# Four transformer layers in one launch: spreads of gates by sixteen strided writes, products finished in the next layer, and transposes through DRAM

## The chip, the cores and the metric

The kernel runs on one core of a Trainium2 chip. Its engines are TensorE (PE: matrix products; PEld is the load of the stationary operand), VectorE (DVE), ScalarE (ACT), GpSimd (POOL) and SyncE (SP, which here issues nearly all DMAs). The metric is the device time of one launch in microseconds, the median over several runs. For this kernel a difference under 0.3%, some 4.2 us, can't be told from none.

## The reference

Eight layers, four of attention and four of feed-forward, act one after another on 4096 tokens of 128 numbers, in float32, each on the normalized tokens, with its result added to them. Cut to what the change touches:

```
x = L0_attn_x                                   # 8 x 512 tokens x 128
x = x + L0_attn(_layernorm(x), ...)
x = x + L0_ffn(_layernorm(x), ...)              # each of 8 heads of 16 numbers picks 2 of 16 experts
x = x + L1_attn(...); x = x + L1_ffn(...)       # linear attention; gated product, 256 chosen tokens
x = x + L2_attn(...); x = x + L2_ffn(...)       # 16 heads, softmax over the queries; 8 low-rank experts
x = x + L3_attn(...); x = x + L3_ffn(...)       # convolution of 21 taps; products of 4-bit numbers

def _L0_ffn_ref(x, ...):
    t = (x @ Wm + bm).reshape(-1, 16)
    topw, topi = top_k(softmax(t @ expert_emb), 2)
    hmid = gelu(einsum('td,edi->tei', t, W1) + b1)
    eo = einsum('tei,eio->teo', hmid, W2) + b2
    return (weighted sum of the two chosen eo).reshape(..) @ Wo + bo

def _L3_attn_ref(x, W1, W2, bias, table):       # 21 taps over time, one filter per channel
    return x @ W1 + causal_conv(x, table) @ W2 + bias

def _L3_ffn_ref(x, w_gate, w_up, w_down):       # fp4: blocks of 16 numbers, rounded to 8 levels
    h = silu(fp4(x) @ fp4(w_gate).T) * (fp4(x) @ fp4(w_up).T)
    return fp4(h) @ fp4(w_down).T
```

## The kernel before

The tokens stay in SBUF as eight blocks `x[0]` to `x[7]` of 512 tokens (four tiles of 128 tokens by 128 features; NB = 8, J = 4, TB = 512, P = 128, D = 128). The order of the instructions on every engine is the order in which the program writes them (`manual_schedule`); nothing is reordered afterwards. An engine that waits holds everything written behind it.

**Layer 0 (0 to 384 us).** After the attention (to about 101 us) come 128 units, one for each block b and expert e, sixteen per block. `first_half(b, e)` makes the hidden numbers: eight products on PE, and the GELU on ACT in two instructions (L569, 512 wide; L570, 1536 wide). `second_half(b, e)` makes eight products from them, DVE multiplies by the gate (L582, `pr`), and POOL adds `pr` to `acc` (L588). The gate of a token for an expert is one row of 512 numbers in DRAM (`gates[b]`); `spread(b, k)` (L550) brings four experts' rows into `gs`, 128 partitions, each head's rows repeated over its 16 partitions: eight DMAs of 128 KB, one per head. `gs` has three buffers, so a spread is issued by `fetch` as soon as four units have been used up. The program keeps eight DMA semaphores for such transfers in turn, so the issue of one waits for the eighth before it. The `choice` of a block (the two best experts and their weights, mostly DVE) runs beside the units of the block before and writes its gates to DRAM by four DMAs (L477). `finish(b)` multiplies the block's sum by `wo` and adds the result to `x[b]`: it is put at the fifth unit of the next block, and for the last block after all units; there the last `pr` goes into the product by itself.

**Layer 1 (384 to about 510 us).** A list of steps with offsets, applied to the blocks in turn (`run`).

**Layers 2 and 3 (516 to 1330 us) in 64 frames.** Frame n is one pair of heads of a block (eight frames per block) of layer 2's attention: `first_scores(n)`, `context(n-1)`, `weigh(n, 0)`, `scores(n, 1)`, `project(n)` (the queries and keys of n+2, the values of n+1 and the output of n-1 in 64-row halves, interleaved), `weigh(n, 1)`. Between two halves of `project`, the order is held by marks: an empty instruction on SP (L1523) that waits for one PE instruction and that another PE instruction waits for. In the frames of the set `moving` (9, 12, 17, 20) the plain 128-row functions `queries`, `output` and `values` stand for `project`. All other work is hung into the frames with `at(frame, hook, function)`. The hooks, in the order in which they run: S and P inside the first scores, V behind them, G behind the first weighing, D before the projections, E at the end. Hung in are the layer-2 experts (`put`, `load`, `products`, `back`, `add`), the norms of layer 2 (`new_xt`), the quantized weights of layer 3 (`rounded`, `turned_w`), and layer 3 block by block (`planned`): norm, 21 taps of the convolution (`conv_v` on DVE, L2009; `conv_s` as a product on ACT, L2023, and a sum on POOL, L2024), `quant_x`, `turn_x`, four gate steps, `quant_h`, `blocks_h` and `fetch_h` (h turned through DRAM, already in the kernel before), `down`. A block is "wide" for b from 0 to 4.

Turning by PE means four transposes into PSUM and a copy by ACT or DVE: `turn_` of `norm_steps` (L1472) for the tokens of layers 2 and 3, `turn_x` (L2089), `turned_w` (weights). `end()` (to 1392 us) does what is left of layer 3's last blocks.

Of the kernel before, what the change touches and what calls it, by code (L numbers as in the profile page):

```python
# [164 lines left out]
def body(ctx, tc, dram, spans, x_in, ib, it, ic, ei, out):  # L165
# [113 lines left out]

    def layer0():  # L280
# [7 lines left out]
        with ExitStack() as st:  # L288
# [7 lines left out]
            acc = once.tile([P, NB, TB], F32, tag="acc", name="acc")  # L296
# [46 lines left out]
            def scale(b, own=3):  # L343
                l0[b]["xn"] = xn = norm.tile([P, J, D], F32, tag="xn", name="xn")
                nb, rs = l0[b]["by"]
                scaled(xn, x[b], (nb, rs), own)
                for j in range(own, J):
                    r1, n1 = rs[:, j : j + 1], nb[:, j : j + 1]
                    nc.gpsimd.tensor_scalar(xn[:, j, :], x[b][:, j, :], r1, n1, ALU.mult, ALU.add)
# [89 lines left out]
            def exponentials(b):  # L439
                nc.scalar.activation(acc[:, b, :], depth[:, b, :], AF.Exp)  # L440

            def choice(b):


                d, ex = by_expert(depth, b), by_expert(acc, b)
# [43 lines left out]
            with (  # L489
# [8 lines left out]
                def run(stages, iterations):  # L498
                    for i in iterations:
# [20 lines left out]
                        (lambda b: scale(b, J), -1),  # L520
# [22 lines left out]
            def spread(b, k):  # L543

                gs = wp.tile([P, 4, TB], F32, tag="gs", name="gs", bufs=3)
                src = gates[b].rearrange("(h k e) t -> k h e t", h=8, k=4)[k]
                n = 2 if (b, k) == (0, 0) else 4
                for e in range(0, 4, n):
                    for hd in range(8):
                        nc.sync.dma_start(  # L550
                            gs[16 * hd : 16 * (hd + 1), e : e + n, :],
                            src[hd, e : e + n, :].unsqueeze(0).to_broadcast([16, n, TB]),
                        )
                return gs
# [18 lines left out]
            def second_half(b, e, hm, gs):  # L573
# [7 lines left out]
                pr = acc[:, b, :] if e == 0 else wp.tile([P, TB], F32, tag="pr", name="pr")  # L581
# [3 lines left out]
                if (b, e) == (NB - 1, 15):  # L585
                    l0[b]["last"] = pr
                elif e > 0:
                    nc.gpsimd.tensor_tensor(acc[:, b, :], acc[:, b, :], pr, ALU.add)  # L588

            def finish(b):  # L590
                terms = [(lambda j: acc[:, b, j * P : (j + 1) * P], f0["wo"])]
                if "last" in l0[b]:
                    terms.append((lambda j: cols(l0[b]["last"], j), f0["wo"]))
                add_to_residual(b, by_token(terms, None))
# [48 lines left out]
            with tc.manual_schedule():  # L643
# [36 lines left out]
                def second(n):  # L680
# [5 lines left out]
                    for _ in range(1 if n > 1 else 5):  # L686
                        side("V", n)

                for n in range(len(units) + 2):
                    first(n)  # L690
                    if n >= len(units):

                        banks["own"] = threes[0][:, 1 + n - len(units), :]
                        second(n)
                        banks.pop("own")
                        continue
# [3 lines left out]
                    if e == 4 and b > 0:  # L700
# [5 lines left out]
                finish(NB - 1)  # L706
# [124 lines left out]
    def layer1():  # L831
# [9 lines left out]
        with tc.tile_pool(name="l1", bufs=2) as wp, tc.tile_pool(name="l1c", bufs=1) as once:  # L841
# [372 lines left out]
            def chosen_put():  # L1214
# [13 lines left out]
                (project_kv, 0),  # L1228
                (z_turn, -7),
# [9 lines left out]
            with tc.manual_schedule():  # L1239
# [13 lines left out]
                nought = once.tile([P, J, D], F32, tag="nought", name="nought")  # L1253
# [152 lines left out]
    def late():  # L1406
# [11 lines left out]
        with tc.tile_pool(name="a2", bufs=2) as wp, tc.tile_pool(name="l3", bufs=1) as lp:  # L1418
# [3 lines left out]
            steps = {}  # L1422

# [6 lines left out]


            def norm_steps(b, dst, bias=None, part=(0, J)):
# [41 lines left out]

                return stats, scale, turn_, t
# [223 lines left out]
            class Rows:  # L1699
# [116 lines left out]
                def products(self, meanwhile, ahead):  # L1816
# [63 lines left out]
                    def last(k, d):  # L1880
# [11 lines left out]
                        for m, f in enumerate((nc.scalar.copy, nc.vector.tensor_copy)):  # L1892
# [33 lines left out]
                def back(self, js):  # L1926
                    if js[0] == 0:
                        self.rows = both("cg").rearrange("p (n d) -> p n d", d=D)
                    for j in js:
                        for k in range(2):  # L1930
                            n = 2 * j + k
                            at_ = 8 * self.b + n
                            nc.gpsimd.indirect_dma_start(
                                self.rows[:, n, :],
                                None,
                                slots_out[self.b],
                                bass.IndirectOffsetOnAxis(spots[:, at_ : at_ + 1], 0),
                            )
# [49 lines left out]
            def layer3(b, xp, tile_, part=(0, J), conv_bank="one", h_tag="h"):  # L1988
# [96 lines left out]

                def turn_x():
# [58 lines left out]
                def quant_h2_tile(i, j):  # L2145
                    sc, a = t["fh", i]
                    k = slice(22 * j, 22 * (j + 1))
                    h = tile_("h", h_tile)
                    fp4_round(lp, h[:, 2 * i + j, :], sc[:, k], a[:, k, :], 22)
# [76 lines left out]
                stats, scale, turn_, _ = norm_steps(  # L2226
                    b, lambda: xp()[:, pad + lo : pad + hi], "b3", part
                )
                stats2, scale2, _, t2 = norm_steps(b, None, None, part)
                return SimpleNamespace(t=t, **{k: v for k, v in locals().items() if callable(v)})  # L2230

            def planned(b, f0_):
# [7 lines left out]
                plan = [  # L2240
                    (1, "V", s.stats) if b == 1 else (0, "E", s.stats),
                    (1, "G", s.scale),
                    (1, "E", s.turn_),
                    (2, "D", lambda: s.conv_v(5)),
                ]
                if b == 0:
# [6 lines left out]
                        (3, "E", lambda: s.conv_s(15, 16)),  # L2253
                        (4, "E", lambda: s.conv_s(19, 20)),
                    ]
                else:
                    plan += [
                        (2, "V", lambda: s.conv_v(1, 2)),
                        (3, "V", lambda: s.conv_v(3, 4)),
                        (2, "G", lambda: s.conv_s(6, 7)),  # L2260
                        (2, "E", lambda: s.conv_s(8, 9, 10)),
                        (3, "G", lambda: s.conv_s(11, 12)),
                        (3, "E", lambda: s.conv_s(13, 14, 15)),
                        (4, "G", lambda: s.conv_s(16, 17)),
# [7 lines left out]
                    (6, "E", s.quant_x1) if early else (z - 2, "V", s.quant_x1),  # L2272
                    (z - 1, "V", s.quant_x2),
                    (z - 1, "E", s.turn_x),
                ]
                for j in range(J):
# [10 lines left out]
                    (h_ + 4, "V", lambda: s.quant_h2(1)),  # L2287
                ]
                if wide:
                    plan += [  # L2290
                        (z + 2, "E", lambda: s.blocks_h(0)),
                        (z + 3, "E", lambda: s.fetch_h(0)),
                        (z + 4, "E", lambda: s.blocks_h(1)),
                        (z + 5, "E", lambda: s.fetch_h(1)),
                        (z + 6, "E", s.down),
# [12 lines left out]
            for b in range(1, NB):  # L2308
                stats, scale, turn_, _ = norm_steps(b, new_xt(b), "lb")
                n = {1: 3, 2: 6, 3: 14, 4: 26, 5: 33, 6: 40, 7: 47}[b]  # L2310
                at(n, "V" if b < 4 else "E", stats)
                at(n + 1, "G", scale)
                at(n + 1, "E", turn_)
            start = [13, 20, 27, 34, 41, 48, 56]
            rows_after = {}
            for b in range(2):
# [10 lines left out]
                at(8 * b + 11, "E", lambda r_=r_: r_.back((0, 1)))  # L2327
                at(8 * b + 12, "G", lambda r_=r_: r_.back((2, 3)))
# [9 lines left out]
            def end():  # L2338
# [63 lines left out]
                B.quant_h2_tile(1, 0)  # L2402
                B.quant_h2_tile(1, 1)
# [5 lines left out]
            def weights_in_frames():  # L2409
# [20 lines left out]
                def turned_w(name):  # L2430
                    ps = bank()
                    w_ = wq[name]
                    if name == "down":
                        for i, at_ in thirds:
                            nc.tensor.transpose(
                                ps[:C3, i * P : (i + 1) * P], w_[:, at_ : at_ + C3], ident
                            )
                        wt["down"] = const.tile([P, 3, P], F32, tag="wd", name="wd")
                        nc.vector.tensor_copy(
                            wt["down"][:C3], ps[:C3, : 3 * P].rearrange("p (i n) -> p i n", i=3)  # L2440
# [237 lines left out]
```

## Time and profile before

| what | us |
|---|---|
| runs (three) | 1394.31, 1395.56, 1398.51 |
| median | 1395.56 |
| the profiled execution | 1393.95 |
| its span, first to last instruction | 1392.2 |
| layer 0 to the last unit's products | 0 to 383.6 |
| layer 1 | 386 to about 510 |
| 64 frames | 516 to 1330 |

The profiled execution is 1.7 longer than its span and 1.6 under the median. Reading: the busy table gives each engine's busy time and share of the span; the chain is followed back from the last instruction; a group's row has line, engine, operation, output and inputs, shape and count, then busy time, mean ns, and the idle time before it with what ended it. A window's row has start:end, length, the busy time of PE, PEld, DVE, ACT and POOL with instruction counts, the granted clock, the share of the DMA engines and GB/s. A timeline's row has start, duration, engine, line, operation, and in square brackets the idle time before and what ended it.

### The profile page before, as it was taken

Reading aid. Unit: us, or ns where it says so; the run is one execution under the profiler, and the core shown is the slowest. Engines: PE = TensorE matmul, PEld = TensorE weight load, DVE = VectorE, ACT = ScalarE, POOL = GpSimd, SP = SyncE. Lnnn points to the kernel's source line nnn. Section 1 sums busy time; section 2 is a strip of 40 time slices with the busy share of each in tenths; the row PEclk is TensorE's granted clock in tenths of the full one; section 3 lists DMA queues with packets and bytes.
Section 4 is the critical chain, followed back from the end, with each engine's and each line's share of the span. In section 5 each row is a group of like instructions: output and inputs, shape, how many; then the busy total and the mean of one; then the engine's idle time right before and its main releaser. Section 6 shows DMA issues by size and latency. Waiting matters only on the chain.

```text
span 1392.2 us, 33106 instructions
## 1 busy us (share of the span) xinstructions
PE 1327.5 (95%) x12935; PEld 706.1 (51%) x12935; DVE 1014.3 (73%) x2148; ACT 1014.6 (73%) x2060; POOL 642.4 (46%) x748
## 2 busy tenths in 40 slices
PE   7889999999989999999999999999999999999997
PEld 3762222222267655547447545555555545555576
DVE  6785556666467778863783778888788797887876
ACT  7869999999978656665684686787767867667632
POOL 6645666666632533330472353353443634424432
PEclk9999999999999999999999999999999999999999
DMA  5019999999681010031211101101011010010000
GB/s 180 1 27 139 141 126 127 132 127 133 85 272 32 28 40 24 16 108 33 60 31 38 45 2 22 30 2 33 20 22 24 9 33 20 19 27 9 2 8 16
DMA packets 100713, 78.14 MB, mean 56 GB/s; under 512 B 52717, under 2 KB 93581, under 8 KB 96206
## 3 DMA queue, kind: packets, MB, share of 16 engines
q1 hardware_dynamic: 98828, 72.10, 28.3%
q0 software_dynamic: 1152, 2.36, 0.6%
q8 instruction: 102, 1.67, 0.6%
q10 hardware_dynamic: 578, 1.57, 0.3%
q14 instruction: 53, 0.43, 0.1%
HBM read 59.03 MB, written 16.97 MB: 55 GB/s over the span
## 4 chain that ended last, share of the span: by engine, by line
PE 52%; ACT 22%; DVE 19%; issue 3%; POOL 2%; DMA 1%; SPq 1%; DVEq 0%; ACTq 0%; POOLq 0%
PE ps L250 41%; PE ps L1556 8%; ACT hm L570 6%; ACT ex L1635 5%; DVE nm L1629 5%; ACT hm L569 3%; ACT prod L2023 2%; PE ps L2206 1%; DVE fa L1395 1%; DVE acc L2009 1%; DVE s L732 1%; ACT h L389 1%; DVE fa L1379 1%; DVE fsc L1374 1%; ACT q L1517 1%
## 5 line engine op out<-in xcount | busy, mean ns | idle before, releaser
L1635 ACT ACTIVATE ex<-ps,nm 128x512 f32<-128x512 f32 x512 | 345.2, 687 | 172.6 <-DVE nm L1629 170.2
L1629 DVE TENSOR_REDUCE nm<-ps 128x2 f32<-128x1024 f32 x256 | 301.1, 1211 | 41.9 <-PE ps L250 41.5
L250 PE MATMUL ps<-q,k 64*64 64x512 f32 (+1 forms) x2240 | 258.3, 565 | 7.4 <-ACT ex L1635 5.4
L250 PE MATMUL ps<-ex,vs 128*64 128x512 f32 x1024 | 233.9, 599 | 1.1 <-DVE sm L1649 1.1
L1650 POOL TENSOR_TENSOR vs<-v,sm 128x256 f32<-128x256 f32 x128 | 78.6, 614 | 296.6 <-DVE sm L1649 269.6
L588 POOL TENSOR_TENSOR acc<-acc,pr 128x512 f32<-128x512 f32 x119 | 165.6, 1391 | 93.8 <-DVE pr L582 85.8
L1556 PE MATMUL ps<-xt,blob_a 64*64 64x512 f32 x912 | 207.8, 589 | 0.5 <-SPq L1523 0.5
L570 ACT ACTIVATE hm<-ps,blob_f 128x1536 f32<-128x1536 f32 x128 | 196.2, 1533 | 0.0
L582 DVE SCALAR_TENSOR_TENSOR pr<-ps,blob_f,gs 128x512 f32<-128x512 f32 x120 | 90.1, 750 | 93.7 <-PE ps L250 72.1
L250 PEld LDWEIGHTS ps<-q,k 64*64 64x64 f32 x2240 | 74.6, 132 | 150.5 <-ACT ex L1635 77.6
L250 PE MATMUL ps<-h,w 32*128 32x512 f32 x1024 | 148.3, 643 | 1.1 <-ACT hm L569 0.6
L250 PEld LDWEIGHTS ps<-ex,vs 128*64 128x64 f32 x1024 | 68.1, 137 | 152.9 <-issue 126.7
L250 PE MATMUL ps<-hm,w 128*32 128x512 f32 x1024 | 136.9, 607 | 2.3 <-DVE pr L582 2.2
L2024 POOL TENSOR_TENSOR acs<-acs,prod 128x512 f32<-128x512 f32 x96 | 124.0, 1292 | 23.9 <-ACT prod L2023 19.4
L1556 PE MATMUL ps<-blob_a,ct 64*64 64x128 f32 x1824 | 118.6, 269 | 0.0
L1556 PE MATMUL ps<-blob_a,xt 64*64 64x128 f32 x1824 | 118.6, 269 | 0.0
L1556 PEld LDWEIGHTS ps<-blob_a,ct 64*64 64x64 f32 x1824 | 106.3, 133 | 0.0
L1635 ACT ACTIVATION_READ_ACCUMULATOR ex<-ps,nm 128x1 f32 x512 | 104.9, 205 | 0.0
L1556 PEld LDWEIGHTS ps<-blob_a,xt 64*64 64x64 f32 x1824 | 103.0, 133 | 0.0
L569 ACT ACTIVATE hm<-ps,blob_f 128x512 f32<-128x512 f32 x128 | 88.0, 687 | 13.3 <-PE ps L250 13.2
L250 PEld LDWEIGHTS ps<-h,w 32*128 32x128 f32 x1024 | 41.0, 184 | 109.1 <-ACT hm L569 100.5
L1556 PEld LDWEIGHTS ps<-xt,blob_a 64*64 64x64 f32 x912 | 61.7, 133 | 32.2 <-issue 28.7
(373 smaller groups left out, 2204.5 us busy)
## 6 DMA issues: line engine op xcount, KB each, us to landing
gs<-gates SPq DMA_DIRECT2D x248, 128.0 KB, 7.4
ht<-turned_h SPq DMA_DIRECT2D x20, 180.0 KB, 3.0
turned_h<-hb SPq DMA_DIRECT2D x40, 88.0 KB, 2.3
blob_f<-in_f SPq DMA_DIRECT2D x1, 2560.0 KB, 9.0
blob_a<-in_a SPq DMA_DIRECT2D x1, 2056.0 KB, 13.5
x<-in_x SPq DMA_DIRECT2D x8, 256.0 KB, 5.8
gates<-turned SPq DMA_DIRECT2D x32, 64.0 KB, 4.7
slots_in<-nought SPq DMA_DIRECT2D x8, 256.0 KB, 4.8
```

Source lines behind the costliest of these rows:

```text
L250: nc.tensor.matmul(out_, lhs, rhs, start=start, stop=stop)
L389: nc.scalar.activation(hk, hk, AF.Sigmoid, bias=bi[:, k : k + 1], scale=sc[:, k : k + 1])
L569: nc.scalar.activation(hm[:, 0, :], p1, AF.Gelu, bias=bias)
L570: nc.scalar.activation(hm[:, 1:, :], p3, AF.Gelu, bias=bias)
L582: nc.vector.scalar_tensor_tensor(pr, po, f0["b2"][:, e : e + 1], gs, ALU.add, ALU.mult)
L588: nc.gpsimd.tensor_tensor(acc[:, b, :], acc[:, b, :], pr, ALU.add)
L1556: ins = nc.tensor.matmul(*args, **kw).ins
L1629: nc.vector.tensor_reduce(nm, ps, AX.X, ALU.max, negate=True)
L1635: nc.scalar.activation(ex[kt][:, i, :], ps[:, i, :], AF.Exp, bias=nm[:, i : i + 1], accum_out=sm[:, kt, i : i + 1],)
L1650: nc.gpsimd.tensor_tensor(vs[:, tiles, :, :], vs_[n][:, tiles, :].rearrange("p j (i n) -> p j i n", i=2), sm[:, tiles, :].unsqueeze(3).to_ ...
L2023: nc.scalar.activation(p, src, AF.Copy, scale=w)
L2024: nc.gpsimd.tensor_tensor(t["acs"], t["acs"], p, ALU.add)
```

## The change

- Layer 0's `spread`: all but the first become sixteen DMAs of 64 KB, the r-th of which writes partitions r, r+16, r+32, ..., one for each head, each with 8 KB.
- `finish` moves out of the units for blocks 2 to 7: block 2's runs behind the last unit, those of blocks 3 to 7 inside layer 1's list; `acc` of these lives in a pool that lasts longer. The last `pr` is added on POOL like the others. At the start one of four normalizations per block moves from ACT to POOL, and fewer side steps run beside the first two units.
- `in_blocks`: DVE transposes 32 by 32 squares of a 128x512 tile in place, four DMAs write the squares to DRAM in turned order, and one DMA fetches the whole. It replaces PE's transposes and ACT's copies for the tokens of layer 2 (seven blocks), the norm of layer 3 for blocks 2 to 4, and `turn_x` of the wide blocks; the three quantized weights are turned in the same manner. That is 18 runs. A new hook F, behind the second weighing and before E, issues the fetches.
- Taps 1, 2 and 5 of the convolution move, in most blocks, from DVE (`conv_v`) to ACT and POOL (`conv_s`): 19 of 30 taps.
- The gathers of the layer-2 experts' rows (`back`) are issued three before the projection, three at the end of that frame and two in the next; frames 11 and 19 join `moving`. The first copy of `ge` is DVE's.
- The wide blocks' quantizations are moved by a frame, part of the second half's with them; `blocks_h(1)`, `fetch_h(1)` and `down` come one or two frames later; `bounds` one earlier.

```diff
+    def finish(b):
+        wo = f0["wo"]
+        add_to_residual(b, by_token([(lambda j: cols(acc[b], j), wo)], None))
...
-            def scale(b, own=3):
+            def scale(b):
...
-                scaled(xn, x[b], (nb, rs), own)
...
+                scaled(xn, x[b], (nb, rs), 3)
...
-                n = 2 if (b, k) == (0, 0) else 4
-                for e in range(0, 4, n):
-                    for hd in range(8):
-                        nc.sync.dma_start(
-                            gs[16 * hd : 16 * (hd + 1), e : e + n, :],
-                            src[hd, e : e + n, :].unsqueeze(0).to_broadcast([16, n, TB]),
-                        )
...
+                else:
+                    for r in range(16):
+                        nc.sync.dma_start(gs[r::16, :, :], src)
...
-                if (b, e) == (NB - 1, 15):
-                    l0[b]["last"] = pr
-                elif e > 0:
...
+                if e > 0:
+                    nc.gpsimd.tensor_tensor(acc[b], acc[b], pr, ALU.add)
...
-                    for _ in range(1 if n > 1 else 5):
+                    for _ in range((4, 2)[n] if n < 2 else 1):
...
+                        if n == len(units):
+                            banks["own"] = threes[0][:, 0, :]
+                            finish(2)
...
-                    if e == 4 and b > 0:
+                    if e == 4 and 0 < b < 3:
...
-                finish(NB - 1)
...
+                (lambda b: b > 2 and finish(b), 3),
...
+            def in_blocks(src):
+                nc.vector.transpose(src, src)
+                far = tc.dram_tile([P, TB], F32, name=f"turned{len(fars)}")
+                fars.append(far)
+                to = far.rearrange("(c r) (j a s) -> a r j c s", c=4, j=J, a=4)
+                for a in range(4):
+                    nc.sync.dma_start(
+                        to[a],
+                        src[32 * a : 32 * (a + 1), :].rearrange("r (j c s) -> r j c s", j=J, c=4),
+                    )
+                return far
...
+                def blocks():
+                    t["far"] = in_blocks(t["xn"].rearrange("p j d -> p (j d)"))
+
+                def fetch():
+                    nc.sync.dma_start(dst(), t["far"])
...
+                def blocks_x():
+                    t["far"] = in_blocks(t["xq"])
+
+                def fetch_x():
+                    t["xt"] = xt = tile_("xt", block("xt3", 2))
+                    nc.sync.dma_start(xt, t["far"])
...
+                if 2 <= b <= 4:
+                    plan = [
+                        (-1, "E", s.stats),
+                        (0, "G", s.scale),
+                        (0, "E", s.blocks1),
+                        (1, "F", s.fetch1),
+                    ]
...
-                        (2, "V", lambda: s.conv_v(1, 2)),
                         (3, "V", lambda: s.conv_v(3, 4)),
-                        (2, "G", lambda: s.conv_s(6, 7)),
+                        (2, "G", lambda: s.conv_s(6, 7, 1)),
...
-                        (3, "G", lambda: s.conv_s(11, 12)),
+                        (3, "G", lambda: s.conv_s(11, 12, 2)),
...
-                        (4, "G", lambda: s.conv_s(16, 17)),
+                        (4, "G", lambda: s.conv_s(16, 17, 5)),
...
+                if wide:
+                    plan += [
+                        (z - 3, "V", s.quant_x1),
+                        (z - 2, "V", s.quant_x2),
+                        (z - 2, "E", s.blocks_x),
+                        (z - 1, "F", s.fetch_x),
+                    ]
...
-                        (z + 3, "E", lambda: s.fetch_h(0)),
-                        (z + 4, "E", lambda: s.blocks_h(1)),
-                        (z + 5, "E", lambda: s.fetch_h(1)),
-                        (z + 6, "E", s.down),
+                        (z + 3, "F", lambda: s.fetch_h(0)),
+                        (z + 5 + more, "F", lambda: s.fetch_h(1)),
+                        (z + 6 + more, "E", s.down),
...
-                n = {1: 3, 2: 6, 3: 14, 4: 26, 5: 33, 6: 40, 7: 47}[b]
+                n = {1: 3, 2: 5, 3: 14, 4: 27, 5: 34, 6: 41, 7: 48}[b]
...
-                at(n + 1, "E", turn_)
+                blocks, fetch = t_["in turn"]
+                at(n + 1, "E", blocks)
+                at(n + 2, "F", fetch)
...
-                at(8 * b + 11, "E", lambda r_=r_: r_.back((0, 1)))
-                at(8 * b + 12, "G", lambda r_=r_: r_.back((2, 3)))
+                at(8 * b + 11, "D", lambda r_=r_: r_.back((0, 1, 2)))
+                at(8 * b + 11, "E", lambda r_=r_: r_.back((3, 4, 5)))
+                at(8 * b + 12, "G", lambda r_=r_: r_.back((6, 7)))
...
-                    at(frame + 1, "E", lambda name=name: turned_w(name))
+                    at(frame + 1, "E", lambda name=name: raw.update({(name, 0): turned_w(name)}))
+                    at(frame + 3, "F", lambda name=name: fetch_w(name, raw[name, 0]))
...
-                moving = {8 * b + k for b in range(2) for k in (9, 12)}
+                moving = {8 * b + k for b in range(2) for k in (9, 11, 12)}
...
+                    hook(n, "F")
                     hook(n, "E")
```

## What was predicted

> **What bounds the kernel now.** I read the busy table first, then the chain that ended last, then windows inside two stages, then timelines of single waits. All times are microseconds.
>
> ```profile
> PE 1327.5 (95%) x12935; PEld 706.1 (51%) x12935; DVE 1014.3 (73%) x2148; ACT 1014.6 (73%) x2060; POOL 642.4 (46%) x748
> ...
> PE 52%; ACT 22%; DVE 19%; issue 3%; POOL 2%; DMA 1%; SPq 1%; DVEq 0%; ACTq 0%; POOLq 0%
> ```
>
> PE is busy 95% of the span and holds half of the chain, but ACT and DVE hold 41%, so the binding engine differs by stage. Windows (start:end, length, then PE, PEld, DVE, ACT, POOL busy, granted clock, DMA share, GB/s) separate layer 0's experts (first two rows) from the frames of layers 2 and 3 (last two):
>
> ```profile
> 220.00:260.00 40.00, 39.69 (x308) 9.76 (x304) 27.43 (x53) 38.59 (x37) 27.25 (x20) 1.00 0.99 130
> 260.00:300.00 40.00, 39.47 (x311) 9.61 (x307) 28.13 (x62) 38.35 (x39) 27.12 (x20) 1.00 0.99 129
> ...
> 880.00:905.00 25.00, 24.46 (x300) 14.81 (x300) 19.13 (x28) 19.28 (x50) 7.68 (x11) 1.00 0.12 32
> 1000.00:1025.00 25.00, 25.00 (x342) 14.44 (x338) 20.33 (x29) 20.06 (x51) 15.49 (x15) 1.00 0.01 2
> ```
>
> In the experts, PE's share counts waiting matmuls; ACT is at 96%, and the DMA engines at 99% with 129 GB/s: two resources are full at once. In the frames PE is full and nothing else is. Clock 1.00 everywhere.
>
> The experts' pace is ACT's pair per unit (a block and an expert, 128 of them); its one gap per block is a `finish`:
>
> ```profile
> L570 ACT ACTIVATE hm<-ps,blob_f 128x1536 f32<-128x1536 f32 x128 | 196.2, 1533 | 0.0
> L569 ACT ACTIVATE hm<-ps,blob_f 128x512 f32<-128x512 f32 x128 | 88.0, 687 | 13.3 <-PE ps L250 13.2
> ...
> 288.82 0.69 ACT L569 ACTIVATE hm<-ps,blob_f 128x512 f32<-128x512 f32 x1 [1.37 <-PE ps L250]
> ...
> gs<-gates SPq DMA_DIRECT2D x248, 128.0 KB, 7.4
> ```
>
> A unit is 2.07 (starts 288.82, 290.88, 292.95); with a finish ahead of it 3.48, so a finish costs 1.41. A block is 16 x 2.07 + 1.41 = 34.5.
>
> In a frame (base 10.64) PE's transposes lie between the last product of one step and the next:
>
> ```profile
> 886.72 0.49 PE L1556 MATMUL ps<-blob_a,xt 64*64 64x128 f32 x6
> 887.31 0.63 PE L1472 MATMUL ps<-blob_c,xn 128*128 128x128 f32 x4
> 887.87 1.95 PE L250 MATMUL ps<-q,k 64*64 64x512 f32 x16
> ```
>
> From the start of the last projection to the next scores is 1.15; where no transposes stand it is 0.32.
>
> **Transposes through DRAM.** Each run takes its PE transposes off the frame's end and adds a VectorE transpose of 128x512 (0.70, by L474, 702 ns), four writes and one or two fetches on SP. On PE, by the gaps around each: seven token runs of layer 2, 0.88 + 0.92 + 0.88 + 0.91 + 0.91 + 1.08 + 1.14 = 6.7; three norms of layer 3 at 1.05 = 3.15; five `turn_x`, 1.08 once and 0.45 four times (after `down`) = 2.9; three weights at 0.68 to 0.70 = 2.1. Together 14.85 for the 18 runs.
>
> What it costs back. (a) `fetch_x` sits at the new hook F, about 1.1 before the frame ends and, in frames 30, 37, 44, 51, behind another fetch of 256 KB on SP; such loads land 2.3 (weights by row) to 3.0 (`ht`) after issue, and the gate step wants the tile 1.34 into the next scores. Stall 0 to 1.1 each: 0 to 4.4, I take 2.5. (b) In frames 28, 35, 42, 49 two runs of writes stand on SP ahead of the marks (L1523) that order the next projection's two halves; DVE's `hb` transpose (0.88 at 876.49) ended about 8.4 into the frame, the mark is wanted at 9. Behind the late mark wait PE's second half, then `v` and the next `ex`. Eight issues of 0.42 to 0.46 are 3.5; 0.6 of cover and four of them already out leave 0 to 1.5 late: 0 to 6, I take 1.5, because the base frame has SP idle before. (c) DVE: 15 x 0.70 added, 19 taps taken off (19 x 0.927 = 17.6, L2009). So DVE gains in sum; but in frames 25 and 48 its instructions add to 13.3 and 13.0 (11.7 before) while PE needs about 11.8 there: 0 to 5, I take 2. (d) The taps go to ACT (0.718, L2023) and POOL (1.292, L2024); ACT's sum per frame rises to 12.1 in a few frames of 11.83, but its measured union is lower: 0 to 2, I take 1. The cover of (c) and (d) is PE's full frame; were it gone, 19 x 0.718 = 13.6 would show. (e) Frames 11 and 19 take the 128-row form (frames 12 and 20, of that kind, measure 11.04 against 10.64): +0.8. (f) Gathers moved around D, E and G: POOL has 4 to 6 idle per frame; 0.
>
> Small gains: the products' first copy `ge` moves to DVE, where ACT's late copy held PE (2.7 + 0.9 waited in two products): 0.9 to 3.6, I take 0.9. Frame 55 has 0.93 of PE gaps behind DVE (11.4 busy of 12.0), and loses two taps: 0.7.
>
> Frames: -14.85 - 0.9 - 0.7 + 2.5 + 1.5 + 2 + 1 + 0.8 = **-8.65**.
>
> **Finishes.** In-stage finishes for blocks 2 to 6 go: 5 x 1.41 = 7.05 if nothing else holds the block. Something does: the spreads, which take 8.16 of DMA per 1 MB (eight DMAs at 1.02) and stand still about 2.1 per block while the choice's weights are written, 4 x 8.16 + 2.1 = 34.7, already the block's length. The slack of a block's first spread before use is only 1.41, 1.74, 2.17 in blocks 4, 6, 7. With unchanged DMA rate the gain is that slack, 2; with faster spreads 7.
>
> **Sixteen-way spreads.** 496 DMAs of 64 KB replace 248 of 128 KB; each now writes partitions r, r+16, ... and has 8 packets of 8 KB instead of 16. SP: 0.465 per issue unblocked (199.77, 200.24, 200.69), 16 x 0.465 = 7.4 per spread, or 64 x 0.465 + 5.1 (choice) = 34.9 per block: as full as the DMA.
>
> ```profile
> SPq L550 <- DMA gs<-gates: 84.8, 129, 1.8
> SPq L550 <- DVE pr L582: 16.2, 13, 2.2
> ```
>
> SP now waits 129 times for an earlier DMA, so issue isn't the limit yet. What a packet will take decides: 0.366 when the queue was empty (200.36), 1.02 once full; the 7200-byte packets that spread one row over all 128 partitions at 12.3 to 14.7 kept 0.273, so rereading one source row isn't what slows them; the write into 16 neighbouring partitions is. A block has 64 such DMAs one after another, so the break-even is 64 x p + 2.1 = 34.7, p = 0.51. Bounds: p = 0.273 x 8192/7200 = 0.31 (then issue binds, full gain -7) and 1.02 (4 x 16.3 + 2.1 = 67.4 per block, +33 in each of 8). Between, half as many packets at a time through the same 128 GB/s give p = 0.512, and I take this one, since the rows show a shared rate: packets lengthened step by step as a queue filled. Stage: **-2**, from -7 to +5 near that value.
>
> [...] The trace shows no 8-packet DMA of this size. [...]
>
> **Layer 1 and the tail.** Five finishes now run inside layer 1: eight matmuls each, 0.89 of PE, in a stage where PE's first iterations have idle of 1.8 to 2.2: 5 x 0.89 = 4.5 less one hidden, **+3.5** (2.5 to 5). After the last unit PE ended at 383.63 and layer 1 began at 386.24, behind `finish(7)` waiting on POOL's sum (start 384.35): **-2.6** (-1.5 to -3.2). The fourth normalization per block on POOL instead of ACT (layer 0's start): 0, between -1 and +1. `bounds` and the layer-3 quantizations a frame earlier lie on DVE beside PE: counted in (c).
>
> **Sum.** -8.65 - 2 + 3.5 - 2.6 = -9.75, on the profiled 1393.95 gives 1384.2. The median of the runs is 1.6 above that execution, so 1385.8: **1386**.
>
> **Rivals.**
> 1. *Full feed and late fetches.* Stage 0, layer 1 +5, tail -2; frames -16.45 + 0.8 with (a) 4.4, (b) 3, (c) 5, (d) 2 = -1.25. Sum +1.75: 1395.56 + 1.75 = **1397**, no change. For: frames 25 and 48, and SP's marks behind eight issues; against: nearly every bound must be at its end. Chance 0.12.
> 2. *Slower side: eight packets at a time.* One mechanism: in the experts' stage, the packet time p on half the packets. Each 0.01 over 0.51 costs 64 x 0.01 = 0.64 per block, 5.1 in eight. At p = 0.53 the whole gain is gone, from 0.54 it is slower; the second DMA of a burst already had 0.576. At 0.55: 8 x (64 x 0.55 + 2.1 - 34.7) = +21 instead of -2, **1409**; at 1.02 some 1650. For: saturated rows show 1.02; against: fewer writers at a time. Chance 0.15.
> 3. *Faster spreads and hidden costs.* Stage -7, (a) to (d) a quarter of what I took (1.75 instead of 7): 1386 - 5 - 5.25 = **1376**. Chance 0.20.
> 4. My forecast: 0.53.
>
> About 0.3% (4.2) is what a measurement of this kernel can tell from no change. Faster: 0.53 and 0.20, 0.73 in all; same 0.12; slower 0.15. The range 1371 to 1404 takes in rivals 1 and 3 and the edge of 2; the likeliest case alone is 1380 to 1392.
>
> **What would show it.** Experts: windows with ACT above 39 of 40 and no 1.37 gaps mean -7; waits of `pr` on DMA of `gs`, and packets over 0.53, mean rival 2. Frames: the gap before first scores 0.32 instead of 1.15; PE idle at L2206 on the fetched tile is (a), at L1556 on SP (b), at L250 scores on DVE `nm` (c). Layer 1 should be about 3.5 longer. I am wrong if the frames together gain less than 3 or the stage moves by more than 7.

## The result, and the profile after

The changed kernel takes 1462.43 us (median of 6 runs, 1461.41 to 1467.46) against 1395.91 before (6 runs, 1394.31 to 1398.51): ratio 1.0482, 95% interval 1.0463 to 1.0500. It is slower by 67, where 1386 and a range of 1371 to 1404 were predicted. Split at the same places in both traces (from the second part of the first unit's GELU to the end of the last unit's products; from there to the first frame; 63 frames, each from its first `ps<-ex,vs` product to that of the next; what follows them). What lies ahead of the first row took 103.7 before and 103.1 after.

| stage, us | before | after | difference | predicted |
|---|---|---|---|---|
| layer 0's units | 279.9 | 341.0 | +61.1 | -2 |
| end of the units and layer 1 | 132.1 | 133.3 | +1.2 | +0.9 |
| frames | 814.2 | 820.3 | +6.1 | -8.65 |
| after the frames | 62.3 | 62.4 | +0.1 | 0 |

The page of the changed kernel, its busy table and the chain that ended last (shares by engine):

```profile
PE 1343.3 (92%) x12738; PEld 701.8 (48%) x12738; DVE 1008.2 (69%) x2165; ACT 1016.2 (70%) x2054; POOL 672.6 (46%) x782
...
PE 37%; DVE 12%; ACT 7%; issue 2%; POOL 1%; DMA 1%; SPq 1%; ACTq 0%; DVEq 0%; POOLq 0%
```

ACT's and DVE's work is what it was, within 7; the span grew by waiting. Two windows of the experts' stage, in the columns of before:

```profile
220.00:260.00 40.00, 32.97 (x248) 7.38 (x244) 18.40 (x30) 31.30 (x31) 22.17 (x17) 0.91 0.38 106
260.00:300.00 40.00, 33.13 (x240) 7.25 (x240) 20.23 (x37) 30.72 (x30) 21.82 (x17) 0.91 0.38 106
```

ACT fell from 38.5 to 31 of 40, so it sets the pace no more. But the DMA engines, at 0.99 before, stand at 0.38: they don't set it either. PE's granted clock fell to 0.91. Next come PE's largest wait in total (us in total, times, longest one) and the DMA engines' row of the page, in tenths of 40 equal slices. The first of the two rows is the kernel before's, with 9 in slices 3 to 9 (counted from 0); the second is the changed kernel's, with 3 in slices 3 to 11:

```profile
PE ps L250 <- DVE acc L593: 38.0, 7, 5.8
```

```profile
DMA  5019999999681010031211101101011010010000
DMA  5013333333337101133122110121211212110000
```

Who waits behind that, in the view of the spread's own line (duration of one issue on SP, ns: least, median, most; then who waited for it, us and times), and in the group of `acc` (which the first unit of each block writes):

```profile
L564 SPq DMA_DIRECT2D gs<-gates x496: 542/543/1278, 105.9 to 433.2; - x166
...
  DVE acc L593: 46.0, 8
  DVE pr L593: 7.5, 7
```

```profile
L593 DVE SCALAR_TENSOR_TENSOR acc<-ps,blob_f,gs 128x512 f32<-128x512 f32 x8 | 6.0, 752 | 46.0 <-DMA gs<-gates 46.0
```

DVE waits 46 for the spreads of eight blocks, 4.5 at the start of the first two and about 6 at each later one, and PE waits for DVE. The table of SP's waits, which had 84.8 for earlier `gs` transfers before, has no row for that any more: the issues simply follow one another, each 0.543 and then 0.044, one every 0.587. Sixteen are 9.4 per spread, and a block takes 64 x 0.587 + 5.1 = 42.7 of SP. The blocks' lengths, between the first GELUs of neighbouring blocks, are 43.0, 42.57, 42.18, 43.05 and 42.55 from block 2 on, against 34.6 to 34.9 before. The sequencer that issues had become the bound; its 42.7 accounts for these lengths without anything for PE's lower clock.

### The profile page after: what moved, and what is told of

Its sections match the earlier page's. It is cut to its first block, busy times and chain, and to the rows that moved or that the text cites. A ratio compares the mean times of both kernels' runs of the same rounds, so it can differ in the third digit from the quotient of the medians.

```text
span 1460.1 us, 33196 instructions
## 1 busy us (share of the span) xinstructions
PE 1343.3 (92%) x12738; PEld 701.8 (48%) x12738; DVE 1008.2 (69%) x2165; ACT 1016.2 (70%) x2054; POOL 672.6 (46%) x782
## 4 chain that ended last, share of the span: by engine, by line
PE 37%; DVE 12%; ACT 7%; issue 2%; POOL 1%; DMA 1%; SPq 1%; ACTq 0%; DVEq 0%; POOLq 0%
PE ps L250 26%; PE ps L1582 9%; ACT ex L1661 4%; DVE nm L1655 4%; PE ps L2239 2%; DMA xt<-turned 1%; SPq L2191 1%; ACT xn L1473 1%; DVE s L1461 1%; DVE fa L1401 1%; DVE fa L1402 1%; DVE v L1529 1%; DVE fm L1400 1%; ACT prod L2049 1%; DVE fa L1385 1%
## 5 line engine op out<-in xcount | busy, mean ns | idle before, releaser
L250 PE MATMUL ps<-q,k 64*64 64x512 f32 (+1 forms) x2240 | 261.3, 567 | 9.7 <-ACT ex L1661 6.9
L1582 PE MATMUL ps<-xt,blob_a 64*64 64x512 f32 x880 | 202.6, 593 | 6.5 <-SPq L1549 6.5
L250 PE MATMUL ps<-hm,w 128*32 128x512 f32 x1024 | 146.1, 644 | 50.4 <-DVE acc L593 38.0
L250 PE MATMUL ps<-h,w 32*128 32x512 f32 x1024 | 156.5, 677 | 1.1 <-ACT hm L580 0.6
L2050 POOL TENSOR_TENSOR acs<-acs,prod 128x512 f32<-128x512 f32 x115 | 147.3, 1281 | 14.3 <-ACT prod L2049 8.6
L1582 PE MATMUL ps<-blob_a,xt 64*64 64x128 f32 x1760 | 115.3, 270 | 0.0
L1582 PE MATMUL ps<-blob_a,ct 64*64 64x128 f32 x1760 | 115.1, 270 | 0.0
L1582 PEld LDWEIGHTS ps<-blob_a,ct 64*64 64x64 f32 x1760 | 102.5, 133 | 0.0
L250 PEld LDWEIGHTS ps<-hm,w 128*32 128x32 f32 x1024 | 20.7, 111 | 152.3 <-DVE pr L593 90.4
```

Source lines behind the costliest of these rows:

```text
L250: nc.tensor.matmul(out_, lhs, rhs, start=start, stop=stop)
L1582: ins = nc.tensor.matmul(*args, **kw).ins
L2050: nc.gpsimd.tensor_tensor(t["acs"], t["acs"], p, ALU.add)
```

## Experiments on layer 0

The lengths below are those of blocks 2 to 6 in each trace (first GELU to first GELU), for which the first two blocks' own delays are over.

**e1_eight**: the changed kernel with the old spread.

```diff
-                    for r in range(16):
-                        nc.sync.dma_start(gs[r::16, :, :], src)
+                    for hd in range(8):
+                        nc.sync.dma_start(gs[16 * hd : 16 * (hd + 1), e : e + n, :],
+                            src[hd, e : e + n, :].unsqueeze(0).to_broadcast([16, n, TB]))
```

> The changed kernel with only the spreads as they were (eight DMAs of 128 KB to 16 neighbouring partitions). Theory A, the spread is issue-bound on SP: in the changed kernel's trace sixteen issues follow one another at a constant 0.587, 9.4 per spread, 42 to 43 per block against 34.7 before; so this undoes nearly all of the loss before the frames (61.6) and the run ends at 1399 to 1406, with units at 2.07 and a PE clock of 1.0 again. Rival B, the finishes in layer 1, the sums' new pool or the changed start of layer 0 are to blame: 1440 or more.

1407.99, ratio to before 1.0100 (1.0077 to 1.0124); blocks 34.49, 33.06, 33.15, 33.61, 35.21. The loss of layer 0 is the spread's. The time is 2 above the expected range: ACT waited 4.9 at the start of block 1, and 1.9 and 2.9 at two later blocks. A window of it shows the DMA engines full again:

```profile
260.00:300.00 40.00, 39.63 (x312) 8.92 (x304) 28.46 (x64) 39.63 (x39) 27.50 (x20) 1.00 0.99 130
```

So without finishes in the way the old spread holds some blocks back, as the prediction had it. Its floor of 34.7 per block was too high, though: blocks 3 to 6 are 3.9 shorter than before, of the 5.6 that four finishes cost, where the prediction allowed 2 for the whole stage.

**e2_before16**: the kernel before with the diff above reversed.

> The kernel before with only the sixteen-way spreads put in. Theory A: 7 to 7.5 blocks, each longer by 42.6 - 34.7 = 7.9, so 1450 to 1458, the finishes hidden under the wait. Rival B: under 1410.

1455.06 (one run; before 1395.34 beside it); units 339.5, frames 814.7. The spread alone makes the loss, with the finishes hidden under it.

**e3_half**: the same sixteen issues, half the bytes.

```diff
-                        nc.sync.dma_start(gs[r::16, :, :], src)
+                        nc.sync.dma_start(gs[r::16, :2, :], src[:, :2, :])
...
```

> The changed kernel with the same sixteen DMAs per spread, each with half the bytes: they bring the gates of two experts of four, and the other two are weighed with the gates of the first two (the output is another for that). Theory A, time by the number of issues: the stage keeps 42 to 43 per block, 1458 to 1465. Rival C, time by bytes (packets on eight engines, or the partitions written): a spread falls from 9.4 to about 5 and the run to 1395 to 1410.

1470.09 (one run), 5 above theory A's range; units 345.1, 4 longer than in the changed kernel, frames 823.7, 3 longer. A window of it:

```profile
260.00:300.00 40.00, 33.47 (x248) 7.35 (x240) 19.62 (x32) 31.47 (x31) 22.65 (x17) 0.91 0.24 57
```

57 GB/s instead of 106, and the same ACT time: half the bytes buy nothing, and rival C falls. Neither the bytes nor the packets' time bound this stage. A spread, which takes 9.4 at 106 GB/s in the changed kernel, takes as long here at 57 GB/s (an issue is 0.543 in both).

**j4_split**: sixteen issues again, contiguous ones, each for one head and two experts.

```diff
-                    for r in range(16):
-                        nc.sync.dma_start(gs[r::16, :, :], src)
+                for e in range(0, 4, 2):
+                    for hd in range(8):
+                        nc.sync.dma_start(gs[16 * hd : 16 * (hd + 1), e : e + 2, :],
+                            src[hd, e : e + 2, :].unsqueeze(0).to_broadcast([16, 2, TB]))
```

> The changed kernel with sixteen contiguous DMAs of 64 KB per spread: each head's 16 partitions, two experts at a time. Theory A1, the issue's cost comes with the strided form (0.587 strided, 0.465 contiguous): 16 x 0.465 = 7.4, so the DMA engines' 8.2 bind again, as in e1_eight: 1400 to 1412. Theory A2, any sixteen issues of 64 KB take 9.4: 1455 to 1470.

1411.66 (one run), units 285.7; one issue every 0.463 in the median. So sixteen issues don't have to cost 9.4: the strided form, with its source of eight rows, does, 0.587 against 0.463. That A1 named the DMA engines as the next bound was wrong, as the window shows:

```profile
260.00:300.00 40.00, 37.67 (x280) 8.13 (x272) 23.74 (x45) 36.27 (x35) 24.90 (x18) 0.96 0.47 121
```

Their share is 0.47 where e1_eight has 0.99. 64 x 0.463 + 5.1 = 34.7 would make SP the bound again; blocks were 33.3 to 37.7. The time also holds frames of 826.5, 6 more than the changed kernel's with the same code.

**e4_doubled**: eight issues of sixteen packets, to every eighth partition; the gates of a block lie twice in DRAM for it.

```diff
-                    for r in range(16):
-                        nc.sync.dma_start(gs[r::16, :, :], src)
...
+                    two = twice[b].rearrange("(u k e) t -> k u e t", u=16, k=4)[k]
+                    for r in range(8):
+                        nc.sync.dma_start(gs[r::8, :, :], two)
```

> The changed kernel with the gates of blocks 1 to 7 doubled in DRAM by one DMA per block, so that a spread is eight DMAs of sixteen packets that write partitions r, r+8, r+16, ...; the choice starts four units earlier; block 0 is spread as before. Theory A: eight issues of 0.47 to 0.59 are 3.7 to 4.7 per spread, well under the 8.3 of four units, so ACT sets the pace: blocks of 33.1, 7 to 12 under e1_eight: 1388 to 1396. If 128 GB/s is a limit whatever partitions are written (rival D), a spread stays at 8.2 and the run within 3 of e1_eight.

1401.25, ratio 1.0041 (1.0023 to 1.0059); blocks 34.78, 33.07, 33.16, 33.07, 33.22: ACT's pace of 16 x 2.07, and each finish that left the units is worth its 1.41.

```profile
260.00:300.00 40.00, 39.98 (x312) 9.23 (x312) 24.25 (x38) 39.96 (x40) 28.40 (x21) 1.00 0.60 158
```

ACT is full at last, and the DMA engines move more than before (158 against 129) in 0.60 of the time, their 8 KB packets 0.31 to 0.65 long where before has 0.98 in the median. Rival D falls: 128 GB/s is no limit for every form. What lifts it is not shown by this run alone, which changes the partitions that one DMA writes and also reads sixteen rows of DRAM in place of one. Sixteen neighbouring partitions alone don't make the long packets: in j4_split, which writes them too, nearly all packets of 4 KB took 0.16 to 0.46 (between 180 and 340), with 121 to 131 GB/s in its windows. An issue of e4_doubled's form took 0.587 and 0.044, more than one of eight packets (0.543), so here the price went with the strided form (j4_split: 0.463 for sixteen contiguous packets), not with the packets being few. The run missed its range since block 1 stood still: DVE waited 5.8 for its first spread.

**g0_steps**: e4_doubled with the side steps back.

```diff
-                    for _ in range((4, 2)[n] if n < 2 else 1):
+                    for _ in range(1 if n > 1 else 5):
```

> e4_doubled with the side steps beside layer 0's first two units back at 5 and 5 (the change has 4 and 2). In e1_eight and e4_doubled ACT stands still for 4.9 and 6.8 at the start of block 1, since DVE waits for that block's first spread. Theory E, the choice of block 1 starts four units late by the fewer steps: the stall goes, blocks 0 and 1 fall by 7 to 8 together, and the run ends near 1391. Rival: the stall comes from the doubling or the order of the finishes, and stays; 1397 to 1401.

1406.72 (one run), above both ranges: units are 281.4, and the stretch from them to the frames is 137.8, the longest of all runs. ACT still stood 7.2 at block 1's start, where DVE waited 5.8 for `gs`. Theory E falls for this kernel; what is left is the doubling, a further trip through DRAM ahead of that block's first spread, on which j1_best bears. That run doubles from block 2 on, has 5 and 5 steps, and waits 0.9 there; e1_eight, with 4 and 2 and no doubling, 4.9, which fits the steps as its cause but wasn't tried alone.

## Experiments on the frames

They all have the doubled spread; the number that counts is that of the frames. With the code of the changed kernel it varies: 820.3 there, 820.2 in e1_eight, 823.7 in e3_half, 826.5 in j4_split, 820.5 in e4_doubled, 819.2 in g0_steps. With the code of before it is 814.2, 814.7 (e2_before16) and 813.3 (g7_frames). So two single runs a few us apart show little by their sums; some single frames repeat far better (28, 35 and 42 take 11.23 or 11.24 in all six runs of the changed frames).

**g1_xpe** (x of the wide blocks on PE: `if wide:` around `blocks_x` and `fetch_x` becomes `if False:`).

> g0_steps with the wide blocks' x turned on PE again (turn_x for blocks_x and fetch_x, quantized a frame later, as before). Theory F, SP's queue: in the changed kernel twelve issues of 0.54 to 0.85 stand ahead of the marks in frames 29, 36, 43 and 50, and the gate step then waits for the fetched x; taking four issues and that fetch away gives these four frames back 2 to 3 each less 0.45 for the transposes: frame 1 to 63 falls from 820.3 to 810 to 814. Rival G, DVE's transposes and the softmax chain behind them hold the frames wherever x is turned: 817 or more.

1398.69 (one run), frames 817.7 against 819.2 for g0_steps. That is rival G's range, not theory F's, and no difference that counts. In frame 29 PE waits 0.7 at L1592 (marks) and 1.2 at `turn_x`, instead of 2.7 in all: x is now quantized on DVE behind the second half of h, which the change moved into the same frames. So this is no clean undoing.

**g3_norms** (the seven norms on PE: `if 2 <= b <= 4:` becomes `if False:`, and for b > 3 `at(n + 1, "E", turn_)` with n of before).

> g0_steps with layer 2's norms of blocks 4 to 7 and layer 3's norms of blocks 2 to 4 turned on PE again, at the places of before; x still goes through DRAM. By the prediction's saving of 0.9 to 1.1 for each of these seven the frames would take 7 more, 827. Theory F: four or eight issues less in the frames 28 to 50 and no late DVE transposes give back as much: 816 to 822. Rival G: under 816.

1394.16 (one run), frames 811.7, as rival G had it. Seven of the prediction's gains, 7.2 in its sum, are a loss of 7.5 when they are made. The sets don't overlap: j1_best and j3_taps below, with the same norms on PE, have 812.8 and 813.2. With these seven on PE the frames are 2.5 shorter than before.

**g7_frames** (all of layers 2 and 3 as before).

> g0_steps with all of layers 2 and 3 as in the kernel before: what is left of the change is layer 0 with doubled gates and the finishes in layer 1. Frames 814.2 as before (by e2_before16, where the frames took 814.7 behind the changed spreads): 1391 - 6 = 1385, against 1395.6 before; layer 1 about 2 longer than before.

1395.42, ratio 0.9996 (0.9984 to 1.0008); frames 813.3. The expected 1385 fails by block 1's stall, 7.6 here, not by the frames, which are those of before.

**j1_best**, **j2_xpe** and **j3_taps**: doubling from block 2 on, steps 5 and 5, norms on PE, gathers as before (`back((0, 1, 2, 3))` at E and `back((4, 5, 6, 7))` at G, `moving` without 11 and 19); then x on PE; then taps 1, 2 and 5 back in `conv_v`.

> The change with doubled gates for blocks 2 to 7 only (blocks 0 and 1 spread as before), side steps 5 and 5, seven norms on PE as in g3_norms, and the gathers and the set moving as before. In g7_frames and g0_steps block 1 waits 6 for its first doubled spread, so without the doubling there the first two blocks return to 35 and 34.5, then 34.5 and 33.07 five times: the stage is 7 shorter than before; layer 1 is 2 longer; the frames are 811.7 (g3_norms) less 1.4 for the gathers, 810.3, against 814.2. Sum 1395.6 - 7 + 2 - 3.9 = 1387 (1384 to 1391). If block 1's wait has another cause than the doubling, 1393 or more.

1389.55, ratio 0.9951 (0.9933 to 0.9970): within the expected 1384 to 1391, and faster than either kernel. Units 274.4, frames 812.8.

> j1_best with x of the wide blocks on PE too (turn_x). Theory F (SP's queue and the late fetch of x): with the norms gone from SP the fetch is in time in frames 43 and 50 but still late by 0.8 to 1.2 in 29 and 36, so PE's transposes cost 5 x 0.45 and save 2: frames within 2 of j1_best. Theory G (VectorE's order): x's transpose no longer ahead of the softmax maxima: frames 3 or more shorter than j1_best.

1391.64 (one run), frames 817.7, 4.9 over j1_best. Both theories miss it. Frames 29, 36, 43 and 50 take 14.32 each, against 12.2 to 13.5 in j1_best, and PE waits 1.1 to 1.2 at `turn_x` in each, by the profile for POOL; g1_xpe has such waits too. What would have to move to end them wasn't tried.

> j1_best with the 19 taps back on DVE. If DVE binds the frames in which the convolution runs (22 to 28, 29 to 35, ...), 19 x 0.927 = 17.6 more on it lengthen the frames by 4 to 12; if PE alone binds them, by less than 2.

1387.36 (one run), frames 813.2 against 812.8, under the expected 2. Nineteen taps on or off DVE make no difference that counts: where they stood, PE covered them.

**k1_pe** to **k4_both** add the two costs of a transpose through DRAM singly to a common base. The function put at the change's place is one of these:

```diff
+                    # k2_dve
+                    nc.vector.transpose(xn, xn)
+                    # k3_sp
...
+                    for a in range(4):
+                        nc.sync.dma_start(to[a],
+                            xn[32 * a : 32 * (a + 1), :].rearrange("r (j c s) -> r j c s", j=J, c=4))
```

> The layer 0 of j1_best and the change's layers 2 and 3, but the seven norms (layer 2's blocks 4 to 7, layer 3's blocks 2 to 4) are turned by PE at the hook F where the change fetches them; no VectorE transpose and no write to DRAM for them. g0_steps has frames of 819.2 with them through DRAM, g3_norms 811.7 with them on PE at the places of before. Both theories: 811 to 815; this is the base of the next three.

> k1_pe plus the seven VectorE transposes of 128x512 at the change's places, in place, with no writes (so PE turns tiles whose squares of 32 are already transposed, and the output differs). Theory G, VectorE's order: each 0.70 stands ahead of the softmax maxima of the next scores, which PE and ACT wait for: 4 or more over k1_pe, the waits on ACT's ex in front of the scores growing by it. Theory F, SP's queue: within 1.5 of k1_pe.

> k1_pe plus the 28 writes to DRAM that the change makes of these seven tiles, at its places on SP, straight from the normalized tile and read by nobody. Theory F: the eight issues of 0.54 to 0.85 in frames 28, 35, 42 and 49 hold the marks of the next projection and the fetch of x behind them: 4 or more over k1_pe, in frames 29, 36, 43 and 50. Theory G: within 1.5 of k1_pe.

> k1_pe plus both (output as in k2_dve): as the change, with PE's transposes in place of the seven fetches. If the two costs add and only move the end of a full PE, k2 and k3's excess in sum, within 2; frames 819 to 828.

| one run each | time | frames | over k1_pe | frames 29 + 36 + 43 + 50 |
|---|---|---|---|---|
| k1_pe | 1391.04 | 814.2 | | 53.07 |
| k2_dve | 1394.82 | 818.2 | +4.0 | 54.98 |
| k3_sp | 1394.6 | 813.5 | -0.7 | 52.53 |
| k4_both | 1397.1 | 819.5 | +5.3 | 55.81 |

(k3_sp's time is longer by its layer 0, where block 2 waited 4.4.) Seven transposes on DVE cost 4.0: 1.9 in the four frames of the last column, and 0.59 in each of frames 28, 35 and 42 ahead of them, in k4_both over k3_sp as well. In those three PE waits for ACT's `ex` as theory G expected, in k2_dve and k4_both alone; in frame 28 of k2_dve:

```profile
879.24 1.09 PE L250 MATMUL ps<-q,k 64*64 64x512 f32 x8 [0.25 <-ACT ex L1676]
```

28 issues on SP, alone, cost nothing; the 1.3 more of both together is within what single runs vary by. So theory G holds for the transposes, and F falls for the writes.

The third part of a transpose through DRAM, its fetch, is in none of the four runs. k4_both's frames, at 819.5, are as long as the changed kernel's, though PE still turns the seven tiles there. Without PE's transposes frames 28, 35 and 42 are 0.81 shorter, but 29, 36, 43 and 50 take 59.99 in the changed kernel and 58.9 to 61.9 in the five others of its code, against 55.81. In frame 29 of the changed kernel SP issues a norm's fetch 0.44 ahead of the fetch of x, for which PE then waits 1.46; in the same four frames of the k runs PE waits for x 0.27 at most. That the fetches cost these 3 to 6 is likely, but no run adds them alone, and g3_norms and j1_best, without them, still wait 0.73 and 0.41 for x, once each.

How a transpose of 0.7 becomes a stall of PE is seen in frame 36, which starts at 973.9 in k1_pe and at 975.0 in k2_dve. The timeline of k1_pe, rows of DVE and then of SP (start, duration):

```profile
972.46 0.68 DVE L1450 STREAM_TRANSPOSE fa<-fa 128x512 f32<-128x512 f32 x1
973.23 2.36 DVE L1670 TENSOR_REDUCE nm<-ps 128x2 f32<-128x1024 f32 x2
...
978.24 0.91 DVE L2202 STREAM_TRANSPOSE hb<-h 128x704 f32<-128x704 f32 x1 [0.91 <-POOL h L1413]
```

```profile
973.16 2.60 SPq L1455 DMA_DIRECT2D turned<-fa  x4
979.18 2.05 SPq L2206 DMA_DIRECT2D turned_h<-hb  x4
981.56 0.34 SPq L2132 DMA_DIRECT2D xt<-turned  x1
```

The same of k2_dve, and its one wait on PE:

```profile
973.56 0.68 DVE L1512 STREAM_TRANSPOSE xn<-xn 128x512 f32<-128x512 f32 x1
974.16 0.67 DVE L1450 STREAM_TRANSPOSE fa<-fa 128x512 f32<-128x512 f32 x1
974.76 2.32 DVE L1670 TENSOR_REDUCE nm<-ps 128x2 f32<-128x1024 f32 x2
...
979.72 0.91 DVE L2202 STREAM_TRANSPOSE hb<-h 128x704 f32<-128x704 f32 x1 [0.90 <-POOL h L1413]
```

```profile
974.86 2.60 SPq L1455 DMA_DIRECT2D turned<-fa  x4
980.66 2.76 SPq L2206 DMA_DIRECT2D turned_h<-hb  x4
983.74 0.34 SPq L2132 DMA_DIRECT2D xt<-turned  x1
```

```profile
983.53 0.65 PE L1597 MATMUL ps<-xt,blob_a 64*64 64x512 f32 x2 [1.20 <-SPq L1564]
```

SP issues the same nine DMAs in both. In k2_dve the added row stands ahead of `fa` and of the maxima `nm`; DVE comes to `hb` (the turned h) 4.7 into the frame instead of 4.3, SP's four writes of it end at 8.4 instead of 7.3, and the mark behind them holds PE for 1.20. Of the 1.1 by which the writes end later, 0.4 is DVE's (`hb` waits for POOL's `h`, and that for `fa`); the other 0.7 is that their issues are longer, 2.76 against 2.05, for a reason that the rows don't show. In the changed kernel both kinds of stall stand in frame 29:

```profile
958.08 0.65 PE L1582 MATMUL ps<-xt,blob_a 64*64 64x512 f32 x2 [1.20 <-SPq L1549]
962.80 0.51 PE L2239 MATMUL ps<-wt_gate,xt 64*64 64x352 f32 x2 [1.46 <-DMA xt<-turned]
```

## Why the prediction was wrong

- **The issue of a strided DMA**: the step that failed. The prediction wrote "SP: 0.465 per issue unblocked [...] 16 x 0.465 = 7.4 per spread", with the price of contiguous DMAs of before. A strided one takes 0.587, and 64 of those with 5.1 for the choice give 42.7 per block instead of 34.9. Eight blocks are some 62, the measured +61.1. It had counted SP as being as full as the DMA engines, and yet gave this price no upper bound, so no rival held the loss. Both of its signs of being wrong came: the frames gained nothing, and the stage moved by far more than 7.
- **The packets**: "What a packet will take decides" was wrong. They took 0.31 to 0.59 in most cases, near the p of 0.51 that was chosen, and halving them changed nothing. Nor is it shown that "the write into 16 neighbouring partitions" slows a packet: j4_split's 4 KB packets to the same partitions took 0.16 to 0.46. Rival 2 had the sign, but its price hung on the wrong resource: at the packets that came it would have given next to no loss. (The second DMA of the burst at 200.36, given there as 0.576, had packets of 0.48 to 0.78.)
- **Finishes**: right. They cost 1.41 each in the units, come back in full where the spread lets them (e4_doubled: 33.07), and e1_eight shows the old spread eating part. The tail's -2.6 and layer 1's +3.5 make +0.9, and +1.2 was measured; that it is so close is partly luck, since that stretch took 132.6 to 137.8 in the runs with the same finishes, against 132.1 before.
- **18 runs of transposes, -14.85**: the price of PE's transposes was right where nothing else was late: frames 2, 3, 4 and 7 gave 0.68, 0.79, 0.88 and 0.92. For the seven norms of frames 27 to 50 "So DVE gains in sum" failed, with the 2 taken for it: a sum over an engine says nothing of the order in it. The transposes stand ahead of the softmax maxima and of `hb`, where 0.7 late is PE's time (k2_dve, +4.0); the taps stood where nothing waited (0.4, j3_taps). The seven cost 7.5 against PE's transposes at their old place; 2.5 of it lies between g3_norms and k1_pe, which turns them on PE at the change's hook, and how the fetches share in the rest is open.
- **(a) and (b)**: right in place, too small in size. Waits on marks in frames 29, 36, 43 and 50 are 1.20, 1.09, 1.93 and 1.04, and on the fetched x 1.46, 1.61 and 0.35: 8.7 against the 4.0 taken. The writes of these tiles took 0.57 to 0.65 each to issue (one 1.41), not 0.42 to 0.46, and twelve writes stood in a row in frame 29, not eight.
- **Gathers and (e)**: 0 and 0.8 were taken. Frames 11 to 20 took 1.3 more in all. Frame 18 alone took 1.5 more; there SP waited for the scattered rows ahead of a mark. j1_best, with gathers and `moving` as before, took 0.8 less there than g3_norms, 0.4 of it in each of frames 11 and 19.

Most of the miss is layer 0's: with the old spread alone the change is 13 slower (e1_eight against 1395.34), with another spread, the norms on PE and the start and gathers of before it is 8 faster (j1_best against 1397.34).

## What to carry to other kernels

A DMA had two prices here, its issue on SP (0.463 contiguous, 0.587 strided) and its packets on the DMA engines (8 KB: 0.98 in the median before, 0.44 after); the change of form changed both, and the first couldn't be read from DMAs of another form. Look at what the engine that issues has left before doubling its count. And count work that is added to an engine by its place in the order, not by that engine's sum: a transpose of 0.7 ahead of values that others wait for cost 0.59 in each of three frames, while 17.6 of taps where nothing waited made no difference that counts.

## What the runs showed of the chip that was not expected

- Issue on SP, one after another: 0.463 for a contiguous 64 KB DMA of sixteen packets (j4_split), 0.587 for eight packets to every 16th partition whether 8 or 4 KB each, 0.632 for sixteen packets to every 8th (e4_doubled).
- Packets of 8 KB in spreads of 128 KB DMAs took 0.98 in the median with sixteen neighbouring partitions and one row (before) and 0.31 to 0.65 with every eighth partition and sixteen rows (e4_doubled). No run separates partitions, rows and bytes under way at a time.
- PE's granted clock fell to 0.5 for 3.41 or 6.83 at a time, once or more in every block of the changed kernel (0.91 in its windows), and in the kernel before once for 3.41 and then at its end. In blocks 1 to 7 of the changed kernel a wait of PE of 4.0 to 5.8 stands beside the fall; the falls at 104.66 and 439.16, and that at 107.14 before, have none over 1.3 near them. What a fall costs wasn't measured by itself.
